# Experts' rows turned by DMA as 16-bit halves, in a mixture-of-experts kernel

## The chip, the cores and the metric

The kernel runs on one core of one Trainium2 chip. The metric is the device time of a run in microseconds; three runs of the kernel before gave 998.57, 999.82 and 1000.01, median 999.82. A core has TensorE (PE; matmuls, into PSUM), VectorE (DVE), ScalarE (ACT), GpSimd (POOL) and SyncE (SP), which here only issues transfers. ScalarE and GpSimd issue transfers as well. All transfers of the core share 16 DMA engines.

## The reference

Inputs are x and ctx, each 8 x 256 tokens of 512 values in float32. Two residual blocks follow one another:

```
x = x + attention(layernorm(x), ctx, ctx)      # 32 heads of 16, keys and values in 8 groups
h = layernorm(x)
logits = h @ gate_w.T                          # 32 experts
w, sel = the 4 largest logits per token, their softmax weights scaled to sum 1
large  = sum over the 4:  w * (silu(h @ Wg) * (h @ Wu)) @ Wd          # inner size 192
small  = sum over the 4:  w * (silu(h @ cWg) * (h @ cWu)) @ cWd       # inner size 128, one per two experts
x = x + large + 0.05 * small
```

The reference computes every expert for every token and weights most results with 0. The kernel computes each expert for the tokens that chose it alone: 2,048 tokens x 4 choices.

## The kernel before, in words

There are two stages, in float32 throughout.

**Attention** (up to about 490 us in the profile) runs over 8 batches of 256 tokens in slots of some 3 us, 16 to a batch. Within a slot TensorE makes a tile of scores (`scores`), the transposed scores of a tile ten slots earlier (`soft`), and one or two steps of other work that a table (`slots`) writes out by hand: projections, mixing of values, the output layer, and for each tile of 128 finished tokens layernorm, router and place in the experts' lists (`finish`). `InOrder` wraps TensorE, VectorE and ScalarE, so that their instructions keep the written order; steps put into `later` are issued at the next slot (`put_off`). In `finish`, `scale` leaves a tile of normed tokens in `row`; a slot later ScalarE's queue stores it to `xn_all` in DRAM, a table of rows from which experts gather, and `turn_h` turns it on TensorE for the router. GpSimd scatters each token's entries (row number, weight) into the lists of its four experts (L601).

**Two experts ahead.** Near the end of attention the two experts with most tokens so far are chosen, and their first 256 tokens of batches 0 to 5 are gathered (`gather_ahead`, L722) and computed (`ahead`) as filling between the last steps of attention. `turn` there turns 128x128 blocks on TensorE into PSUM and copies them to SBUF.

**The experts** (from about 490 us) come one after another, ordered by load, each with a fixed number of tokens (`SHARES`: 128 and 160, then 352 falling to 192). For expert i the steps are:

- `list_of` (L1055) loads the expert's list, `weights_of` loads 1.25 MB `wm` (L1041) and 0.75 MB `sm` (L1049); all are issued by SyncE. Four expert's weights fit (`wts`, four buffers).
- `tokens_of` (L1067) has GpSimd gather the listed rows, 128 to a tile, two or three tiles, into `rows` (three buffers).
- `turned` (L1094) turns the rows on TensorE: four chunks of 128 columns, for each two or three 128x128 blocks side by side in PSUM (`ept`), which VectorE (L1100) and ScalarE (L1098) in turns copy to `exT`. The chunks of expert i+1 are called between the products of expert i (`between` in `inner`).
- `inner` (L1114) makes five products of width w (gate, up, the tail of both, and the small expert's two), each of four matmuls, with Silu on ScalarE and multiplication on VectorE.
- `down` makes the second layer (L1217, L1219, L1222, for last tiles of few tokens L1195 to L1208), scales by the token's weight, and GpSimd adds the rows onto the output in DRAM (L1176). `in_turn` makes an expert's scatter-adds wait for those of the expert before.

The loop asks in iteration i for rows of i+3, weights of i+3 and the list of i+4. Here a scheduler, not the written order, decides how these instructions stand in SyncE's and GpSimd's queues. In the built program SyncE's queue repeats: wm of n, sm of n, list of n+1. A last loop (`For_i`) takes tokens beyond the fixed shares; there are none or few.

Of the kernel before, what the change touches and what calls it, by code (L numbers as in the profile page):

```python
# [10 lines left out]
F32 = mybir.dt.float32  # L11
I32 = mybir.dt.int32
U32 = mybir.dt.uint32
AF = mybir.ActivationFunctionType
# [22 lines left out]
WARM = 24  # L37
MAXT = B * S
NO_ONE = NS * P


class InOrder:
# [23 lines left out]
def xattn_moe(ctx: ExitStack, tc, x, ctxT, wqT, wkT, wvT, wfcT, bfc, gateT, wx, ws, out):  # L66
# [89 lines left out]
    with ExitStack() as att:  # L156
# [329 lines left out]
        def finish(t):  # L486
# [12 lines left out]
            def fc(h):  # L499
                half = slice(h * (E // 2), (h + 1) * (E // 2))  # L500
                pm = ps_m.tile([P, E // 2], F32, tag="pm", name=f"pmf_{t}_{h}")
                for kc in range(KC):
                    pe.matmul(
                        pm,
                        lhsT=box["oT"][:, kc, :],
                        rhs=wfc_sb[:, kc, half],
                        start=(kc == 0),
                        stop=(kc == KC - 1),
                    )
                dve.tensor_tensor(acc[t][:, half], pm, acc[t][:, half], ALU.add)  # L510
                if h == 0:
                    return
                row = box["row"] = a3.tile([P, E], F32, tag="row", name=f"row_{t}")

                def stats():
                    of = statistics(acc[t], f"f{t}")
                    act.dma_start(out=out[NO_ONE + t * P :][:P], in_=acc[t])

                    def scale():
                        scaled(row, acc[t], of)  # L520
                        later.append(
                            lambda: act.dma_start(out=xn_all[NO_ONE + t * P :][:P], in_=row)
                        )

                    later.append(scale)

                later.append(stats)
# [189 lines left out]

        def gather_ahead():
            for n in range(AHEAD):
                rows = [b2.tile([P, E], F32, tag=f"xn{j}", name=f"ahead{n}_{j}") for j in range(2)]  # L720
# [9 lines left out]
                first_ones["rows", n] = rows  # L730

        def ahead(n):


            a, at, b = units[n]
            up, us, wa, wt, wb = first_ones["weights", n]
            rows, li = first_ones["rows", n], first_ones["li", n]
            half = KC // 2
            xT = [ax.tile([P, half, S], F32, tag="acc", name=f"xT_ahead{n}_0")]

# [5 lines left out]
            steps = {}  # L746

            def turn(kc):
                pm = ps_m.tile([P, S], F32, tag="pm", name=f"pmt_ahead{n}_{kc}")
                for j in range(2):  # L750
                    pe.transpose(
                        pm[:, j * P : (j + 1) * P], rows[j][:, kc * P : (kc + 1) * P], ident
                    )
                dst = xT[kc // half][:, kc % half, :]

                if n or kc % 2:
                    act.copy(dst, pm)
                else:
                    dve.tensor_copy(dst, pm)

            def sum_of(name):

# [174 lines left out]
        for s in range(16 * B + LAG + 6):  # L937
# [16 lines left out]
            if s == 18:  # L954
                fill_blanks()

                hold(nc.sync.dma_start(
                    out=lists.rearrange("(e n) c -> e n c", e=NE)[:, :NO_ONE, :], in_=no_one
                ))
                hold(nc.sync.dma_start(  # L960
                    out=lists.rearrange("(e n) c -> e n c", e=NE)[:, NO_ONE : NO_ONE + S, :],
                    in_=no_one[:, :S, :],
                ))
                hold(nc.sync.dma_start(
                    out=xn_all[:NO_ONE, :].rearrange("(j p) r -> p j r", p=P),
                    in_=nothing.unsqueeze(1).to_broadcast([P, NS, E]),
                ))
            if s in do_ahead:
                do_ahead[s]()
# [65 lines left out]
    ps_x = ctx.enter_context(tc.tile_pool(name="ps_x", bufs=2, reuse_waits="tile", space=bass.MemoryType.PSUM))  # L1035
    ps_u = ctx.enter_context(tc.tile_pool(name="ps_u", bufs=3, reuse_waits="tile", space=bass.MemoryType.PSUM))
    ps_y = ctx.enter_context(tc.tile_pool(name="ps_y", bufs=3, reuse_waits="tile", space=bass.MemoryType.PSUM))

    def weights_of(e_r, n, after=None):
        wm = wts.tile([P, 5 * E], F32, tag="wm", name=f"wm_{n}")  # L1040
        load = nc.sync.dma_start(out=wm, in_=wx[bass.ds(e_r, 1), :, :].rearrange("o p n -> (o p) n"))  # L1041
        if after is not None:
            tc.add_manual_dep(
                load.ins, after.ins.name,
                mybir.DependencyInfo(mybir.DependencyClass.Sync, mybir.DependencyReason.DATA),
                reason="the rows before go first",
            )
        sm = wts.tile([P, 3 * E], F32, tag="sm", name=f"sm_{n}")
        loads.append(nc.sync.dma_start(out=sm, in_=ws[bass.ds(e_r, 1), :, :].rearrange("o p n -> (o p) n")))  # L1049
        return wm, sm  # L1050
# [10 lines left out]

    gathers = {}

    def tokens_of(li, n, ns):
        rows = m3.tile([P, NS, E], F32, tag="rows", name=f"rows_{n}")
        for j in range(ns):
            gathers[n] = nc.gpsimd.indirect_dma_start(  # L1067
                out=rows[:, j, :],
                out_offset=None,
                in_=xn_all,  # L1070
                in_offset=bass.IndirectOffsetOnAxis(ap=li[:, j, 0:1].bitcast(I32), axis=0),
            )
        return rows

    def tiles_of(w):

# [7 lines left out]
            lots[j] = "second" if j % 2 else "first"  # L1084
        return list(zip(sizes, lots))

    def turned(n, rows, ns):

        xT = m2.tile([P, KC, NS * P], F32, tag="xT", name=f"exT_{n}")

        def chunk(kc):
            pt = ps_x.tile([P, NS * P], F32, tag="pt", name=f"ept_{n}_{kc}")
            for j in range(ns):
                tensor.transpose(  # L1094
                    pt[:, j * P : (j + 1) * P], rows[:, j, kc * P : (kc + 1) * P], ident
                )
            if kc % 2:
                nc.scalar.copy(xT[:, kc, : ns * P], pt[:, : ns * P])  # L1098
            else:
                nc.vector.tensor_copy(xT[:, kc, : ns * P], pt[:, : ns * P])  # L1100

        return xT, chunk

# [207 lines left out]

    def fetch_weights(i):
        if i < NE:
            held["weights", i] = weights_of(held["expert", i], i, gathers[1] if i == 2 else None)

    def fetch_tokens(i):
        if i < NE:
            held["tokens", i] = tokens_of(held["list", i], i, ns_of[i])

    before = []  # L1320

# [36 lines left out]
    fetch_tokens(0)  # L1358
    with behind(held["lists", 2]):
        fetch_weights(0)  # L1360
    fetch_weights(1)
    fetch_tokens(1)
    fetch_weights(2)
    fetch_list(3)
    tensor = pe
    now = turned(0, held["tokens", 0], ns_of[0])
    for kc in range(KC):
        now[1](kc)

# [8 lines left out]
    for i in range(NE):  # L1378
        if i > 0:
            fetch_tokens(i + 3)  # L1380
        fetch_weights(i + 3)
        fetch_list(i + 4)
        wm, sm = held["weights", i]
        acts = units[i % 2]
        tensor = nc.tensor if i else pe
        if i + 1 < NE:
            then = turned(i + 1, held["tokens", i + 1], ns_of[i + 1])
# [12 lines left out]
    with tc.For_i(0, n_extra, 1) as i:  # L1400
# [4 lines left out]
        )  # L1405
        li = list_of(lists[bass.ds(row_r, P), :], "l", 1)
        wm, sm = weights_of(e_r, "l")
        rows = tokens_of(li, "l", 1)
# [6 lines left out]
        xT, chunk = turned("l", rows, 1)  # L1415
        for kc in range(KC):
            chunk(kc)
        inner("l", xT, wm, sm, units[0], P)
# [73 lines left out]
```

## Time and profile before

| what | value |
|---|---|
| median of the runs | 999.82 us |
| the profiled execution: its time, its span | 1007.55 us, 1005.7 us |
| mean granted TensorE clock over the span | 0.979 |
| TensorE busy | 971.5 us (97%), 5282 matmuls |
| VectorE, ScalarE, GpSimd busy | 414.3 us (41%), 316.0 us (31%), 321.2 us (32%) |
| the experts' turns: matmuls | 308 + 12, 54.1 + 3.0 us busy |
| copies of turned rows out of PSUM, VectorE, ScalarE | 64 each, 31.4 us and 27.1 us |
| gathers of rows | 80, GpSimd 78.6 us |
| scatter-adds to the output | 80, GpSimd 122.4 us |
| moved by DMA | 133.52 MB, mean 133 GB/s |

The profile gives the busy time of each engine; matmuls overlap in TensorE's pipeline, so their busy times add up to more than the time from one start to the next, and what a matmul costs is read from starts. In the timeline each row has its start and its duration in us, the engine (SPq is SyncE's queue of transfers), the line, the operation with what it writes and reads, and in brackets how long the engine sat idle ahead of it and what ended that. In a group of instructions, the figures after the bar are busy us and mean ns of one.

### The profile page before, as it was taken

What the parts mean: (1) busy time and instruction counts of PE and PEld (TensorE: products, weight loads), DVE (VectorE), ACT (ScalarE), POOL (GpSimd) and SP (SyncE); (2) the same over time, 40 slices, a digit from 0 to 9 for tenths busy, and PEclk for the clock granted to TensorE, in tenths of its full rate; (3) what the DMA queues carried; (4) which work ended last, traced back from release to release, by engine and by line L of the source; (5) the groups of instructions that cost most, each with busy time, mean ns of one, the idle gap of its engine ahead of it and who ended that gap; (6) DMA issues with size and microseconds to landing.
All of it is one profiled execution on the core that took longest, in us unless ns stands there. A gap on an engine that the chain in (4) does not pass through costs nothing. (4 is left out here: it accounts for less than half of the span.)

```text
span 1005.7 us, 14200 instructions
## 1 busy us (share of the span) xinstructions
PE 971.5 (97%) x5282; PEld 605.2 (60%) x5282; DVE 414.3 (41%) x958; ACT 316.0 (31%) x573; POOL 321.2 (32%) x333
## 2 busy tenths in 40 slices
PE   8999999999999998999889999999999999999994
PEld 5545555555555554438565556566767677777772
DVE  5655666666676667435212222222323222211220
ACT  2355455554454544422121122121212111111111
POOL 4201040413131303132426353443435434433322
PEclk9999999999999999959999999999999999999997
DMA  5120201011010000241698878676768687777722
GB/s 201 43 81 2 83 4 60 28 43 44 33 54 33 12 34 12 91 162 43 224 378 229 171 212 220 172 222 176 225 181 244 172 230 230 226 210 214 239 37 34
DMA packets 52632, 133.52 MB, mean 133 GB/s; under 512 B 19441, under 2 KB 20850, under 8 KB 48210
## 3 DMA queue, kind: packets, MB, share of 16 engines
q1 hardware_dynamic: 28690, 83.17, 24.1%
q0 software_dynamic: 18976, 40.25, 18.5%
q10 hardware_dynamic: 4896, 9.18, 2.4%
q8 instruction: 42, 0.69, 0.3%
q14 instruction: 28, 0.23, 0.1%
HBM read 104.75 MB, written 27.56 MB: 132 GB/s over the span
## 5 line engine op out<-in xcount | busy, mean ns | idle before, releaser
L52 DVE TENSOR_REDUCE mx<-sc 128x4 f32<-128x1024 f32 x128 | 156.6, 1223 | 79.3 <-PE st L52 67.0
L52 ACT ACTIVATE pT<-st 128x1024 f32<-128x1024 f32 x128 | 131.0, 1024 | 131.9 <-PE st L52 127.1
L1067 POOL DMA_INDIRECT rows<-xn_all,li x80 | 78.6, 983 | 235.6 <-DMA li<-lists 140.8
L52 PE MATMUL sc<-kT,qT 32*128 32x512 f32 x512 | 144.3, 640 | 5.9 <-DVE mx L52 5.4
L52 PE MATMUL st<-qT,k 32*128 32x512 f32 x512 | 148.0, 655 | 0.0
L1176 POOL DMA_INDIRECT out_dram<-y,li x80 | 122.4, 1530 | 70.2 <-ACT y L1174 40.5
L601 POOL DMA_INDIRECT lists<-ent,slot_i x64 | 62.5, 977 | 115.4 <-DVE slot_i L52 87.8
L1174 ACT ACTIVATE y<-py,li 128x512 f32<-128x512 f32 (+1 forms) x33 | 22.7, 687 | 182.0 <-PE py L1222 173.7
L1172 DVE TENSOR_SCALAR y<-py,li 128x512 f32<-128x512 f32 (+3 forms) x29 | 21.8, 750 | 116.6 <-PE py L1222 112.7
L1100 DVE COPY exT<-ept 128x384 f32<-128x384 f32 (+2 forms) x64 | 31.4, 491 | 90.5 <-PE ept L1094 80.4
L52 PEld LDWEIGHTS sc<-kT,qT 32*128 32x128 f32 x512 | 38.3, 182 | 44.6 <-DVE mx L52 21.2
L52 PE MATMUL po<-pT,va 128*32 128x512 f32 x512 | 65.0, 627 | 0.0
L52 PE MATMUL pmq<-xT,wq_sb 128*128 128x256 f32 x256 | 63.8, 392 | 0.8 <-DVE xT L52 0.8
L1114 PE MATMUL pu_g<-exT,wm 128*128 128x240 f32 (+10 forms) x248 | 63.9, 400 | 0.0
L52 PEld LDWEIGHTS pmq<-xT,wq_sb 128*128 128x128 f32 x256 | 46.0, 189 | 29.5 <-issue 23.5
L52 PE MATMUL pmf<-wfc_sb,oT 128*128 128x256 f32 x256 | 63.0, 391 | 0.0
L52 PEld LDWEIGHTS pmf<-wfc_sb,oT 128*128 128x128 f32 x256 | 46.2, 189 | 26.6 <-issue 15.2
L1114 PE MATMUL pu_ug<-exT,wm 128*128 128x240 f32 (+10 forms) x248 | 61.7, 393 | 0.0
L1114 PE MATMUL pu_u<-exT,wm 128*128 128x240 f32 (+10 forms) x248 | 60.9, 388 | 0.0
L1114 PE MATMUL pu_us<-exT,sm 128*128 128x240 f32 (+10 forms) x248 | 60.6, 387 | 0.0
L1114 PE MATMUL pu_gs<-exT,sm 128*128 128x240 f32 (+10 forms) x248 | 60.6, 387 | 0.0
L1219 PE MATMUL py<-sm,b 128*128 128x512 f32 x124 | 58.7, 593 | 0.3 <-DVE b L1142 0.3
(270 smaller groups left out, 1338.3 us busy)
## 6 DMA issues: line engine op xcount, KB each, us to landing
wm<-in_wx_dram SPq DMA_DIRECT2D x32, 1280.0 KB
sm<-in_ws_dram SPq DMA_DIRECT2D x32, 768.0 KB
out_dram<-acc ACTq DMA_DIRECT2D x16, 256.0 KB
xn_all<-row ACTq DMA_DIRECT2D x16, 256.0 KB
acc<-in_x_dram SPq DMA_DIRECT2D x15, 256.0 KB
ctx<-in_ctxT_dram SPq DMA_DIRECT2D x7, 512.0 KB
rows<-xn_all,li POOLq DMA_INDIRECT x80
out_dram<-y,li POOLq DMA_INDIRECT x80
```

The source lines that it names most:

```text
L52: this = instruction(*args, **kwargs)
L601: nc.gpsimd.indirect_dma_start(out=list_views[TOPK * t + k], out_offset=bass.IndirectOffsetOnAxis(ap=slot_i[:, k : k + 1], axis=0), in_=en ...
L1067: gathers[n] = nc.gpsimd.indirect_dma_start(out=rows[:, j, :], out_offset=None, in_=xn_all, in_offset=bass.IndirectOffsetOnAxis(ap=li[:, j ...
L1100: nc.vector.tensor_copy(xT[:, kc, : ns * P], pt[:, : ns * P])
L1114: tensor.matmul(pu[:, :w], lhsT=cols(kc), rhs=xT[:, kc, :w], start=(kc == 0), stop=(kc == KC - 1),)
L1172: nc.vector.tensor_scalar(y[:m], py[j][:m], weight(j)[:m], None, ALU.mult)
L1174: nc.scalar.activation(y[:m], py[j][:m], AF.Copy, scale=weight(j)[:m])
L1176: nc.gpsimd.indirect_dma_start(out=out, out_offset=bass.IndirectOffsetOnAxis(ap=li[:m, j, 0:1].bitcast(I32), axis=0), in_=y[:m], in_offset ...
L1219: nc.tensor.matmul(py[i], lhsT=b[:, s], rhs=wb, start=False, stop=False)
```

## The change

Everywhere that rows of experts are turned, DMA now does it. The DMA transposition handles 16-bit elements, so a float32 row is kept as its 512 lower halves followed by its 512 upper halves. Turned, each half is a matrix of its own, and a copy that writes with a stride of two 16-bit elements joins them to float32 again. Part by part:

- Router: ScalarE splits each tile of normed tokens (`split`, 128 x 1,024 16-bit elements) ahead of the store to `xn_all`, which becomes a table of 16-bit elements of the same size. `row` has two buffers, not three.
- Experts: `turn_halves` has SyncE issue one transposing transfer for each tile of rows, SBUF to SBUF, for w rows in all. `chunk` becomes one join from `halves` to `exT`, by VectorE and ScalarE in turns. TensorE's turns, PSUM between and their copies go.
- Gathers fetch the w rows of the share, not whole tiles of 128. `rows` has two buffers, `halves` two.
- The loop asks in iteration i for the turn of i+2, after the weights of i+3 and the list of i+4.
- The third expert's weights no longer wait for the second one's gathers by a dependency of their own.
- PSUM: one bank for turns in place of two, four for results in place of three.
- The two experts ahead are turned in the same way.

In the built program of the changed kernel, SyncE's queue repeats from the eighth expert on: wm of n, sm of n, list of n+1, the two or three turns of n+1, wm of n+1.

```diff
+def halves_of(a):
+    return a.bitcast(U16).rearrange("p (n two) -> p two n", two=2)
+
+def joined(copy, dst, turned, kc):
+    copy(halves_of(dst), turned.rearrange("p (two c) n -> p c two n", two=2)[:, kc])
...
-    xn_all = nc.dram_tensor("xn_all", (B * S + NO_ONE, E), F32, kind="Internal").ap()
+    xn_all = nc.dram_tensor("xn_all", (B * S + NO_ONE, 2 * E), U16, kind="Internal").ap()
...
-        a3 = att.enter_context(tc.tile_pool(name="a3", bufs=3))
+        a3 = att.enter_context(tc.tile_pool(name="a3", bufs=2))
...
-                        later.append(
-                            lambda: act.dma_start(out=xn_all[NO_ONE + t * P :][:P], in_=row)
-                        )
+                        def split():
+                            halves = a3.tile([P, 2 * E], U16, tag="halves", name=f"split_{t}", bufs=1)
+                            act.copy(
+                                halves.rearrange("p (two n) -> p two n", two=2), halves_of(row)
+                            )
+                            act.dma_start(out=xn_all[NO_ONE + t * P :][:P], in_=halves)
+                        later.append(split)
...
+                turned = first_ones["turned", n] = aq.tile(
+                    [P, 2 * KC, S], U16, tag=f"qT{n}", name=f"turned_ahead{n}"
+                )
+                for j in range(2):
+                    nc.sync.dma_start(
+                        out=turned[:, :, j * P : (j + 1) * P], in_=rows[j], transpose=True
+                    )
...
-                pm = ps_m.tile([P, S], F32, tag="pm", name=f"pmt_ahead{n}_{kc}")
-                for j in range(2):
-                    pe.transpose(
-                        pm[:, j * P : (j + 1) * P], rows[j][:, kc * P : (kc + 1) * P], ident
-                    )
...
+                copy = act.copy if n or kc % 2 else dve.tensor_copy
+                joined(copy, xT[kc // half][:, kc % half, :], halves, kc)
...
+    mh = ctx.enter_context(tc.tile_pool(name="mh", bufs=2, reuse_waits="tile"))
...
-    ps_x = ctx.enter_context(tc.tile_pool(name="ps_x", bufs=2, ...
+    ps_x = ctx.enter_context(tc.tile_pool(name="ps_x", bufs=1, ...
...
-    ps_y = ctx.enter_context(tc.tile_pool(name="ps_y", bufs=3, ...
+    ps_y = ctx.enter_context(tc.tile_pool(name="ps_y", bufs=4, ...
...
-    def tokens_of(li, n, ns):
-        rows = m3.tile([P, NS, E], F32, tag="rows", name=f"rows_{n}")
-        for j in range(ns):
+    def tokens_of(li, n, w):
+        rows = mh.tile([P, NS, 2 * E], U16, tag="rows", name=f"rows_{n}")
+        for j, (m, _) in enumerate(tiles_of(w)):
             gathers[n] = nc.gpsimd.indirect_dma_start(
-                out=rows[:, j, :],
+                out=rows[:m, j, :],
...
+    def turn_halves(rows, n, w):
+        halves = mh.tile([P, 2 * KC, NS * P], U16, tag="halves", name=f"halves_{n}")
+        for j, (m, _) in enumerate(tiles_of(w)):
+            nc.sync.dma_start(
+                out=halves[:, :, j * P : j * P + m], in_=rows[:m, j, :], transpose=True
+            )
+        return halves
...
         def chunk(kc):
-            pt = ps_x.tile([P, NS * P], F32, tag="pt", name=f"ept_{n}_{kc}")
-            for j in range(ns):
-                tensor.transpose(
-                    pt[:, j * P : (j + 1) * P], rows[:, j, kc * P : (kc + 1) * P], ident
-                )
-            if kc % 2:
-                nc.scalar.copy(xT[:, kc, : ns * P], pt[:, : ns * P])
-            else:
-                nc.vector.tensor_copy(xT[:, kc, : ns * P], pt[:, : ns * P])
+            copy = nc.scalar.copy if kc % 2 else nc.vector.tensor_copy
+            joined(copy, xT[:, kc, :w], halves[:, :, :w], kc)
...
         fetch_weights(i + 3)
         fetch_list(i + 4)
+        turn_tokens(i + 2)
```

More of the change, by code (lines that the diff above doesn't have):

```diff
@@ L13 @@
 U32 = mybir.dt.uint32
+U16 = mybir.dt.uint16
 AF = mybir.ActivationFunctionType
@@ L719, in gather_ahead @@
             for n in range(AHEAD):
-                rows = [b2.tile([P, E], F32, tag=f"xn{j}", name=f"ahead{n}_{j}") for j in range(2)]
+                rows = [
+                    b2.tile([P, 2 * E], U16, tag=f"xn{j}", name=f"ahead{n}_{j}") for j in range(2)
+                ]
                 for j in range(2):
@@ L729, in gather_ahead @@
                     )
-                first_ones["rows", n] = rows
+                turned = first_ones["turned", n] = aq.tile(
[5 more added lines that the diff above has]
+                    )
         def ahead(n):
@@ L736, in ahead @@
             up, us, wa, wt, wb = first_ones["weights", n]
-            rows, li = first_ones["rows", n], first_ones["li", n]
+            halves, li = first_ones["turned", n], first_ones["li", n]
             half = KC // 2
@@ L748, in turn @@
             def turn(kc):
-                pm = ps_m.tile([P, S], F32, tag="pm", name=f"pmt_ahead{n}_{kc}")
-                for j in range(2):
-                    pe.transpose(
-                        pm[:, j * P : (j + 1) * P], rows[j][:, kc * P : (kc + 1) * P], ident
-                    )
-                dst = xT[kc // half][:, kc % half, :]
-                if n or kc % 2:
-                    act.copy(dst, pm)
-                else:
-                    dve.tensor_copy(dst, pm)
+                copy = act.copy if n or kc % 2 else dve.tensor_copy
+                joined(copy, xT[kc // half][:, kc % half, :], halves, kc)
             def sum_of(name):
@@ L965, in xattn_moe @@
                     out=xn_all[:NO_ONE, :].rearrange("(j p) r -> p j r", p=P),
-                    in_=nothing.unsqueeze(1).to_broadcast([P, NS, E]),
+                    in_=nothing.bitcast(U16).unsqueeze(1).to_broadcast([P, NS, 2 * E]),
                 ))
@@ L1032, in xattn_moe, with weights_of @@
     m2 = ctx.enter_context(tc.tile_pool(name="m2", bufs=2, reuse_waits="tile"))
+    mh = ctx.enter_context(tc.tile_pool(name="mh", bufs=2, reuse_waits="tile"))
     m3 = ctx.enter_context(tc.tile_pool(name="m3", bufs=3, reuse_waits="tile"))
     m6 = ctx.enter_context(tc.tile_pool(name="m6", bufs=6, reuse_waits="tile"))
-    ps_x = ctx.enter_context(tc.tile_pool(name="ps_x", bufs=2, reuse_waits="tile", space=bass.MemoryType.PSUM))
+    ps_x = ctx.enter_context(tc.tile_pool(name="ps_x", bufs=1, reuse_waits="tile", space=bass.MemoryType.PSUM))
     ps_u = ctx.enter_context(tc.tile_pool(name="ps_u", bufs=3, reuse_waits="tile", space=bass.MemoryType.PSUM))
-    ps_y = ctx.enter_context(tc.tile_pool(name="ps_y", bufs=3, reuse_waits="tile", space=bass.MemoryType.PSUM))
-    def weights_of(e_r, n, after=None):
+    ps_y = ctx.enter_context(tc.tile_pool(name="ps_y", bufs=4, reuse_waits="tile", space=bass.MemoryType.PSUM))
+    def weights_of(e_r, n):
         wm = wts.tile([P, 5 * E], F32, tag="wm", name=f"wm_{n}")
[L1041 to L1046, printed above, removed]
-            )
+        nc.sync.dma_start(out=wm, in_=wx[bass.ds(e_r, 1), :, :].rearrange("o p n -> (o p) n"))
         sm = wts.tile([P, 3 * E], F32, tag="sm", name=f"sm_{n}")
@@ L1062, in xattn_moe @@
     gathers = {}
-    def tokens_of(li, n, ns):
-        rows = m3.tile([P, NS, E], F32, tag="rows", name=f"rows_{n}")
-        for j in range(ns):
+    def tokens_of(li, n, w):
+        rows = mh.tile([P, NS, 2 * E], U16, tag="rows", name=f"rows_{n}")
+        for j, (m, _) in enumerate(tiles_of(w)):
             gathers[n] = nc.gpsimd.indirect_dma_start(
-                out=rows[:, j, :],
+                out=rows[:m, j, :],
                 out_offset=None,
                 in_=xn_all,
-                in_offset=bass.IndirectOffsetOnAxis(ap=li[:, j, 0:1].bitcast(I32), axis=0),
+                in_offset=bass.IndirectOffsetOnAxis(ap=li[:m, j, 0:1].bitcast(I32), axis=0),
             )
         return rows
+    def turn_halves(rows, n, w):
[5 more added lines that the diff above has]
+        return halves
     def tiles_of(w):
@@ L1085, in tiles_of, with turned @@
         return list(zip(sizes, lots))
-    def turned(n, rows, ns):
+    def turned(n, halves, w):
         xT = m2.tile([P, KC, NS * P], F32, tag="xT", name=f"exT_{n}")
         def chunk(kc):
-            pt = ps_x.tile([P, NS * P], F32, tag="pt", name=f"ept_{n}_{kc}")
-            for j in range(ns):
-                tensor.transpose(
-                    pt[:, j * P : (j + 1) * P], rows[:, j, kc * P : (kc + 1) * P], ident
-                )
-            if kc % 2:
-                nc.scalar.copy(xT[:, kc, : ns * P], pt[:, : ns * P])
-            else:
-                nc.vector.tensor_copy(xT[:, kc, : ns * P], pt[:, : ns * P])
+            copy = nc.scalar.copy if kc % 2 else nc.vector.tensor_copy
+            joined(copy, xT[:, kc, :w], halves[:, :, :w], kc)
         return xT, chunk
@@ L1313, in fetch_weights, with turn_tokens @@
         if i < NE:
-            held["weights", i] = weights_of(held["expert", i], i, gathers[1] if i == 2 else None)
+            held["weights", i] = weights_of(held["expert", i], i)
     def fetch_tokens(i):
         if i < NE:
-            held["tokens", i] = tokens_of(held["list", i], i, ns_of[i])
+            held["tokens", i] = tokens_of(held["list", i], i, SHARES[i])
+    def turn_tokens(i):
+        if i < NE:
+            held["halves", i] = turn_halves(held["tokens", i], i, SHARES[i])
     before = []
@@ L1360, in xattn_moe @@
         fetch_weights(0)
+    turn_tokens(0)
     fetch_weights(1)
     fetch_tokens(1)
+    turn_tokens(1)
     fetch_weights(2)
@@ L1365, in xattn_moe @@
     tensor = pe
-    now = turned(0, held["tokens", 0], ns_of[0])
+    now = turned(0, held["halves", 0], SHARES[0])
     for kc in range(KC):
@@ L1386, in xattn_moe @@
         if i + 1 < NE:
-            then = turned(i + 1, held["tokens", i + 1], ns_of[i + 1])
+            then = turned(i + 1, held["halves", i + 1], SHARES[i + 1])
             inner(i, now[0], wm, sm, acts, SHARES[i], then[1])
@@ L1407, in xattn_moe @@
         wm, sm = weights_of(e_r, "l")
-        rows = tokens_of(li, "l", 1)
+        rows = tokens_of(li, "l", P)
         ed = m1.tile([P, 1], F32, tag="led", name="led")
@@ L1414, in xattn_moe @@
         )
-        xT, chunk = turned("l", rows, 1)
+        xT, chunk = turned("l", turn_halves(rows, "l", P), P)
         for kc in range(KC):
```

## Prediction

> **What bounds the kernel now.** I read the profile in this order: the 40 slices of the span, the groups of instructions, then the timeline of one expert on TensorE, SyncE and GpSimd. The slices first (busy tenths, granted TensorE clock, DMA share):
>
> ```profile
> PE   8999999999999998999889999999999999999994
> PEclk9999999999999999959999999999999999999997
> DMA  5120201011010000241698878676768687777722
> ```
>
> TensorE is full from end to end. The DMA engines are idle in attention (the first 19 slices) and 60 to 80% busy in the experts' stage (from about slice 20, 490 us), full only at its start. The chain of waits is cut off after 2 us and tells nothing. The group to be removed, and the stage (TensorE's busy time, weight loads, DVE, ScalarE, GpSimd, clock, DMA share, GB/s):
>
> ```profile
> L1094 PE MATMUL ept<-ident,rows 128*128 128x128 f32 x308 | 54.1, 275 | 2.4 <-DMA rows<-xn_all,li 2.4
> ```
>
> ```profile
> 700.00:800.00 100.00, 100.00 (x534) 66.74 (x532) 26.80 (x66) 19.49 (x48) 43.03 (x34) 1.00 0.71 203
> ```
>
> 100 of 100 us: here a turn saved on TensorE is time saved. One expert of 288 tokens, TensorE first, then SyncE's queue, then GpSimd:
>
> ```profile
> 706.38 0.49 PE L1094 MATMUL ept<-ident,rows 128*128 128x128 f32 x3
> 706.71 2.11 PE L1114 MATMUL pu_u<-exT,wm 128*128 128x288 f32 x8
> ```
>
> ```profile
> 706.55 0.33 SPq L1041 DMA_DIRECT2D wm<-in_wx_dram  x1
> 707.24 0.18 SPq L1049 DMA_DIRECT2D sm<-in_ws_dram  x1
> 709.86 0.01 SPq L1055 DMA_DIRECT2D li<-lists  x1
> 722.96 0.33 SPq L1041 DMA_DIRECT2D wm<-in_wx_dram  x1
> ```
>
> ```profile
> 717.54 1.02 POOL L1067 DMA_INDIRECT rows<-xn_all,li  x1 [7.55 <-DMA li<-lists]
> 718.87 0.98 POOL L1067 DMA_INDIRECT rows<-xn_all,li  x1 [0.30 <-issue]
> 720.15 0.95 POOL L1067 DMA_INDIRECT rows<-xn_all,li  x1 [0.30 <-issue]
> 721.41 1.62 POOL L1176 DMA_INDIRECT out_dram<-y,li  x1 [0.30 <-issue]
> ```
>
> Two things are to be seen. Three turns push the next matmul back by only 706.71 - 706.38 = 0.33 us, 0.109 each; the 275 ns of the group overlap. And SyncE issues one expert's two weight loads (2 MB) and the next expert's list, then waits for nothing but a free weight buffer. The list lies behind the weights: it lands 717.54 - 706.55 = 11.0 us after wm's issue, and GpSimd gathers then. That latency is no bound today, since SyncE does not wait for it.
>
> **What is removed.** 308 + 12 turns of experts x 0.109 = 34.8 us of TensorE. 24 of them (experts 0 to 2) lie at 494 to 518 us, where TensorE waits for rows and weights anyway, so 296 x 0.109 = 32.2 us could show. The 16 turns of the two experts taken ahead fill waits of TensorE for DVE's routing; I take 1 us. Gathers shrink from 80 x 128 = 10,240 rows to 8,352, 3.9 MB less.
>
> **What is added, off the path.** The joins handle twice as many elements (608 for 304 tokens). ScalarE's rows (0.48 us for 384, 1.02 for 1,024 elements) give about 0.67 us for 0.48, DVE's (0.56 for 384, 1.22 for 1,024) about 0.78 for 0.56. DVE and ScalarE are 27% and 19% busy and a join is needed only by the next expert: nothing. Without that cover it would be 128 x 0.2 = 26 us. The split in attention is 16 copies of 1,024 elements on ScalarE, 1.02 us each by the exponential's row. In the slot where it falls ScalarE has 0.5 to 1 us idle and is half busy over attention; bounds 0 and 16 us, and I take 2, because the copies behind it are read a slot or more later. The turns of the ahead experts are behind their weights, which land by 437 us; TensorE needs them at 451: nothing, or up to 5 us if a turn is dear. PSUM is only regrouped (8 banks as before): nothing.
>
> **What is added on the path: a wait in SyncE's queue.** In the built order of the changed kernel, SyncE's queue from the eighth expert's weights on repeats: wm and sm of expert n, list of n+1, *two or three turns of n+1*, wm of n+1. The turn of n+1 waits for n+1's gather, that for n+1's list, and the list lies behind wm and sm of n. So the next weights are no longer released by a free buffer but by a ring of latencies. (With rows and halves two deep, a turn also waits for the joins of n-1, and a gather for the turns of n-1; both are done a ring earlier. The wait that holds the third expert's weights behind a gather goes, but the turns ahead of them wait for the same gather. On GpSimd the gather of n+1 stands ahead of the scatter-adds of n-3; six result tiles cover that.) The ring:
>
> - wm to the landing of the list: 11.0 us above; in other experts 11 to 14 (754.89 to 768.51, 859.91 to 872.18). The higher ones have gathers of the same moment in them, which the ring now puts before wm; the scatter-adds still overlap. I take 10.8 (10.5 with two tiles), and 0.5 for turns still ahead in the queue.
> - list to the last gather's landing: the third is issued at +3.56 us (721.10 - 717.54); from the end of an issue to the landing I take the routing scatter's 2.45 us (issue ends 398.56, its waiter starts at 401.01). First gather +3.5, second +4.8, third +6.0.
> - the turns themselves, X us for 128 x 1,024 halves (256 KB). No row shows one. Below: a plain issue, 0.33 us. Above: the Trainium skill, "VectorE: DVE Perf Modes", The three transpose paths, puts a 128x128 turn of 16-bit data at 1309 ns by DMA against 390 on TensorE; eight blocks are 10.5 us. This rule speaks against the change doubly, since the trace has TensorE at 109 ns a block, not 390. At 1309 ns in series 8,352 rows would be 65.25 x 8 x 1.309 = 683 us, more than the whole stage of 510. "DMA: Bandwidth & Descriptors", Latency and other measured facts, says 261 GB/s for such transposes: 1.0 us a piece, 17.1 MB in 65 us, and 0.71 share of DMA has room for it. A lone transfer's 1309 ns hold its latency (over 2 us in the rows here), so they are hardly a rate; I estimate X = 1.5, near the bandwidth figure, with 0.33 and 10.5 kept.
>
> With X = 1.5 the turns of three tiles start at +3.5, +5.0, +6.5 (the last short) and end at +7.1: ring = 10.8 + 0.5 + 7.1 + 0.3 for SyncE's own steps = 18.7 us. Two tiles: 10.5 + 0.5 + 6.4 + 0.3 = 17.7. TensorE alone would need 16.6 - 1.3 = 15.3 and 13.7 - 0.8 = 12.8. The ring is longer than either, so it sets the pace once the lead of four weight buffers is eaten (about two experts' time).
>
> Its sum: wm of the eighth expert (566 before) goes out at about 574, because its turn waits for joins in the fifth expert. Then 11 rings of three tiles and 13 of two: 574 + 206 + 230 = 1010 for the last weights (941 before). They land 9 us later[...]; the last expert took from 980.2 to the end at 1005.7, 25.5, now 24.5. End: 1043.5, less 1 from the ahead experts, plus 2 from the split: 1044.5 of span. The profiled execution is 1007.55 us for a span of 1005.7, and the median of the runs, 999.82, is 7.7 below it: 1044.5 + 1.85 - 7.7 = 1039, rounded to 1040. What is late next is TensorE, for weights at each expert's first product.
>
> **Rivals.**
>
> *The ring is short enough (not slower).* If list and gathers land faster, since the DMA engines now have idle time within each ring, TensorE stays the bound. Place: wm to the list. The ring decides at 16.5 us on average ((971 - 574) / 24 makes the last expert start where it does now); at 15.2 the whole 32 us show. With X = 0.33 and the list after 9 us the rings are 15.8 and 14.3. Then span 1005.7 - 32.2 - 1 + 2 + 3 for the crowded start = 977.5, median 972. For it: my latencies come from crowded moments. Against it: no wm of the trace had its list in under 11 us.
>
> *Turns are dear.* With X = 3.2 (the geometric middle of 1.0 and 10.5, some 80 GB/s) the rings are 22.5 and 20.9: 574 + 10 for the start + 247 + 272 + 33.5 = 1137, median about 1131. With 10.5 they are 38 and 34, over 1450. For it: the 1309 ns. Against: the bandwidth figure.
>
> *ScalarE's split stalls attention* at its full 16 us with everything else as forecast: 1054. Against: idle time around it.
>
> *The change does not do what it says*: TensorE keeps no expert turn in the built program, so this is out.
>
> **How the numbers follow.** Ring with X of 0.7 to 2 (1010 to 1065): 0.45. Dear turns (1075 and up): 0.25, of it 0.10 above 1150. Ring about even with TensorE: 0.05 within 0.2% (some 2 us, about what a measurement of this kernel tells from no change) and 0.05 just above. TensorE-bound (970 to 997): 0.20, of it 0.10 below 980. So 980 to 1150 leaves out 0.2; faster 0.20, same 0.05, slower 0.75.
>
> **What would show it.** Right: SyncE's waits name the gather (DMA rows) ahead of the turns; distances from wm to wm are 17 to 19 us from the eighth expert on and equal list plus gather plus turns; TensorE falls below 9 tenths from about 650 us on, waiting for DMA wm at an expert's first product; the DMA share falls though bytes rise. Wrong on the ring: wm still waits for TensorE's last product of an expert. Wrong on X: successive turns of one expert start much more, or less, than 1.5 us apart. Wrong on the split: the end of attention moves by over 5 us.

## The result, and the profile after

The changed kernel takes 1089.52 us (median of 4 runs, 1083.95 to 1094.28), the kernel before 999.2 in the same comparison: the ratio is 1.0902, with a 95% interval of 1.0849 to 1.0955. The prediction said slower and 1040; the time is inside its range, but the loss is more than twice the forecast one (90 us for 40). The profiled execution took 1088.9 us, for a span of 1087.1. Of the 42 runs of the kernel before beside the experiments, 7 took 1005.5 to 1008.2 us and the others 997.7 to 1001.8, and the profiled execution of before (1007.55) is one like the 7.

The slices of the changed kernel, to be laid beside those of before (busy tenths, granted clock, DMA share; a slice is 27.2 us here):

```profile
PE   8999999999999999987879999978878878887774
PEclk9999999999999998998889999999899989888888
DMA  5120102020200005439998886876786878686862
```

Up to slice 26, about 700 us, TensorE is as full as before outside the start of the experts' stage. From there on it never is again. In the window of 700 to 800 us (TensorE, weight loads, DVE, ScalarE, GpSimd, clock, DMA share, GB/s) it works 79.55 of 100 us, where it worked 100, its granted clock is 0.90 for 1.00, and the DMA share is 0.76 for 0.71:

```profile
700.00:800.00 100.00, 79.55 (x364) 51.56 (x361) 19.77 (x54) 17.67 (x39) 34.36 (x28) 0.90 0.76 186
```

One expert in SyncE's queue, from its weights to the next one's, and the gathers on GpSimd that lie between (start, duration in us):

```profile
747.23 0.52 SPq L1062 DMA_DIRECT2D wm<-in_wx_dram  x1
747.94 1.31 SPq L1064 DMA_DIRECT2D sm<-in_ws_dram  x1
750.77 0.39 SPq L1070 DMA_DIRECT2D li<-lists  x1
762.43 5.06 SPq L1094 DMA_TRANSPOSE halves<-rows  x3
767.75 0.48 SPq L1062 DMA_DIRECT2D wm<-in_wx_dram  x1
```

```profile
758.84 1.02 POOL L1082 DMA_INDIRECT rows<-xn_all,li  x1 [11.66 <-DMA li<-lists]
760.16 0.98 POOL L1082 DMA_INDIRECT rows<-xn_all,li  x1 [0.30 <-issue]
761.45 0.86 POOL L1082 DMA_INDIRECT rows<-xn_all,li  x1 [0.30 <-issue]
```

This is the ring of the prediction, closed: wm at 747.23, the list behind it lands at 758.84, gathers, three turns from 762.43 to 767.49, and only then the next wm at 767.75, 20.5 us later. Before, the next wm came 16.4 us after the last (706.55 to 722.96). The waits tell the same. In SyncE's queue, and on the other engines (engine, line, what was waited for: us in total, times, longest):

```profile
SPq L1094 <- DMA rows<-xn_all,li: 265.1, 31, 13.4
```

```profile
ACT exT L50 <- DMA halves<-rows: 297.8, 26, 15.9
POOL rows L1082 <- DMA li<-lists: 268.6, 25, 13.4
DVE exT L50 <- DMA halves<-rows: 250.8, 26, 14.2
...
PE pu_gs L1131 <- ACT sg L1139: 79.8, 20, 7.6
```

SyncE waits for gathers, GpSimd for lists, and ScalarE and VectorE for turned rows, each for over 250 us: one circle. TensorE's own wait is named last. It stands at its fourth product (`pu_gs`), since that needs a PSUM buffer which ScalarE's Silu has to empty, and this Silu stands behind a join that waits for turned rows. The weights themselves are never late. SyncE, for its part, hardly waits for TensorE: 4.9 us in all for weight buffers that TensorE still reads.

What a turn does to SyncE's queue is read from its line (count: least, median, most ns):

```profile
L1094 SPq DMA_TRANSPOSE halves<-rows x80: 1204/1399/5926, 485.5 to 1041.4; - x80
```

And what the turns cost the DMA engines is read from the queue that SyncE fills (packets, MB, share of 16 engines' time):

```profile
q1 hardware_dynamic: 101730, 101.33, 32.3%
```

Before, it had 28,690 packets, 83.17 MB and 24.1%. So 18.2 MB more take 73,040 packets of 249 bytes, and 0.323 x 1087.1 - 0.241 x 1005.7 = 109 us of all 16 engines.

### The profile page after: what moved, and what is told of

Its sections match the earlier page's. It is cut to its first block, busy times and chain, and to the rows that moved or that the text cites. A ratio compares the mean times of both kernels' runs of the same rounds, so it can differ in the third digit from the quotient of the medians.

```text
span 1087.1 us, 13724 instructions
## 1 busy us (share of the span) xinstructions
PE 964.4 (89%) x4946; PEld 591.5 (54%) x4946; DVE 406.9 (37%) x958; ACT 347.3 (32%) x589; POOL 322.3 (30%) x333
## 5 line engine op out<-in xcount | busy, mean ns | idle before, releaser
L63 ACT ACTIVATE pT<-st 128x1024 f32<-128x1024 f32 x128 | 131.3, 1025 | 119.5 <-PE st L63 119.3
L1131 PE MATMUL pu_gs<-exT,sm 128*128 128x240 f32 (+10 forms) x248 | 86.8, 510 | 79.8 <-ACT sg L1139 79.8
L50 ACT COPY exT<-halves 128x480 uint16<-128x480 uint16 (+11 forms) x64 | 45.2, 771 | 306.1 <-DMA halves<-rows 297.8
L50 DVE COPY exT<-halves 128x480 uint16<-128x480 uint16 (+11 forms) x64 | 25.9, 458 | 250.8 <-DMA halves<-rows 250.8
L1131 PEld LDWEIGHTS pu_gs<-exT,sm 128*128 128x128 f32 x248 | 59.1, 249 | 101.3 <-ACT sg L1139 88.0
L1131 PE MATMUL pu_us<-exT,sm 128*128 128x240 f32 (+10 forms) x248 | 68.4, 424 | 0.0
L1131 PEld LDWEIGHTS pu_us<-exT,sm 128*128 128x128 f32 x248 | 54.5, 222 | 12.8 <-issue 0.4
```

Of the source, the lines that this page charges most:

```text
L50: copy(halves_of(dst), turned.rearrange("p (two c) n -> p c two n", two=2)[:, kc])
L63: this = instruction(*args, **kwargs)
L1131: tensor.matmul(pu[:, :w], lhsT=cols(kc), rhs=xT[:, kc, :w], start=(kc == 0), stop=(kc == KC - 1),)
```

## The experiments

The theory: the ring of latencies in SyncE's queue (weights, list, gather, turn, next weights) takes the time. Its rivals: joins that stand in order on ScalarE and VectorE ahead of work for TensorE; DMA engines that the turns fill; the turning itself. Each experiment is one edit to the changed kernel, unless it says otherwise. The runs of before beside them have medians of 999.7 to 1000.5.

**The turn moved behind the next weights and list.**

```diff
-        turn_tokens(i + 2)
+        with behind(held["lists", min(i + 4, NE - 1)]):
+            turn_tokens(i + 2)
```

> The changed kernel, with each expert's turns held in SyncE's queue where the loop writes them: the turn of i+2 after the weights of i+3 and the list of i+4. Its gather is then an expert old when SyncE comes to it. Ring theory (the next weights wait for list, gather and turn of the same expert, 20.6 us a round with three tiles and 17.7 with two): the ring is gone, TensorE is the bound again, less its turns: 965 to 985 us. Bandwidth theory (the turns' small packets fill the DMA engines): still 1040 us or more, DMA share near 1 through the experts' stage. In-order theory (joins stand ahead of Silu in ScalarE's order and stop TensorE): 1060 us or more.

Measured: 1017.8 us (1012.47 to 1023.35), ratio 1.0173 [1.0148, 1.0197]. Of the loss of 90 us, 72 are gone with an edit that changes nothing but the place of the turns in one queue. SyncE's wait for gathers falls from 265.1 to 31.2 us, and wm waits for TensorE again. So the ring carries most of the loss. But 18 us are left and TensorE's saving does not show; none of the three expectations gave this time. The reading that offered itself, DMA engines full of turns (their share was 1.12 to 1.15 from 550 to 900 us), is tried below with turns that nobody waits for, and full engines alone do not give the 18 us.

**Plain copies in place of turns**, in the same place, with the same bytes and the same wait. The rows are not turned, so the kernel computes with wrong rows.

```diff
-            nc.sync.dma_start(
-                out=halves[:, :, j * P : j * P + m], in_=rows[:m, j, :], transpose=True
-            )
+            move = nc.sync.dma_start(
+                out=halves[:, :, j * P : j * P + m],
+                in_=rows[:, 0, :].rearrange("p (c n) -> p c n", n=P)[:, :, :m],
+            )
+            tc.add_manual_dep(move.ins, gather_of[n][j].ins.name, ...
```

> The changed kernel with each experts' turn replaced by a plain copy of the same size from SBUF to SBUF, issued by SyncE at the same place and after the same gather; the rows are not turned (the computation leaves that out, and takes all tiles from the first one). Ring theory: only the turns' issue time leaves the ring, some 2.2 us of 20.6 with three tiles and 1.6 of 17.7 with two, and their data ahead of the weights some 0.5: 1025 to 1045 us, so most of the loss stays. Bandwidth theory, or one in which turning by itself is what costs: 1000 us or less.

Measured: 1042.85 us (1041.42 to 1043.28), ratio 1.0429 [1.0413, 1.0445]. The ring is there without any turning (SyncE waits 196.5 us for gathers), and it costs 43 us. The other 47 come with the turning. A plain copy holds SyncE's queue 0.61 us (median), a turn 1.40, so one would expect 11 rings of three tiles x 2.4 us and 13 of two x 1.6, together 47. The sum meets the total, but by luck: of the 46 us between the two spans 13.9 lie ahead of the eighth expert's weights, 11.5 in the eleven rings of three tiles (19.5 us each for 20.5), 19.5 in the thirteen of two (16.3 for 17.8) and 1.0 at the end.

**All joins written behind the fifth product**, so that no Silu should stand behind a join.

```diff
-        between(0)
...
-        between(3)
...
+        for kc in range(KC):
+            between(kc)
```

> The changed kernel with the four joins of the next expert put after an expert's fifth product, not between its products, so that no Silu stands behind a join that waits for its turn. Ring theory: the wait only moves to the next expert's first product and the pace stays; at the end the last but one expert need not wait for the last turn, 8 to 10 us: about 1080 us. In-order theory: the stall goes, 1000 to 1020 us.

Measured: 1089.92 us, ratio 1.0905 [1.088, 1.0929], no difference from the changed kernel. But the edit did not reach the engines. In the built program the joins stand where they stood: from 485 us on ScalarE's 222 instructions and VectorE's 289 come in the same order as in the changed kernel. The next expert's joins (544 elements) still stand ahead of this expert's Silu (288), and TensorE waits 81.2 us for it, where it waited 79.8:

```profile
731.24 1.46 ACT L50 COPY exT<-halves 128x544 uint16<-128x544 uint16 x2 [12.31 <-DMA halves<-rows]
...
734.02 0.41 ACT L1139 ACTIVATE sg<-pu_g 128x288 f32<-128x288 f32 x1
```

So this run is the changed kernel once more and does not test the rival. What speaks against it lies elsewhere. The members of the ring hardly wait for the engines that compute (SyncE 4.9 us in all for TensorE to free weight buffers and 7.4 for ScalarE, GpSimd's scatter-adds 10.2 for ScalarE), and the kernel with the list first and ten buffers, below, has the joins in the same place ahead of the Silu and runs at TensorE's pace. TensorE's wait for ScalarE is where the delay is felt, not where the pace comes from. The 8 to 10 us that a later join might save at the end stay untested.

**The list asked for ahead of the weights.**

```diff
-        fetch_weights(i + 3)
         fetch_list(i + 4)
+        fetch_weights(i + 3)
```

> The changed kernel with the list of i+4 asked for ahead of the weights of i+3, so that no list lies behind 2 MB of weights; the turns still stand ahead of the next weights in SyncE's queue. Ring theory: the largest term of the ring (11.7 us from the weights to the list's landing) falls to 2 or 3, the ring to 11 to 14 us, below TensorE's 12.8 to 15.3: 965 to 990 us. Bandwidth theory: still 1040 us or more. In-order theory: 1060 us or more.

Measured: 1046.05 us (1041.76 to 1053.53), ratio 1.0452 [1.0427, 1.0477]: half of the loss is back, where the ring theory had wanted all. SyncE's largest wait in the experts' stage shows why:

```profile
SPq L1070 <- DMA out_dram<-y,li: 239.5, 30, 11.9
```

The list now waits for one of six list buffers, which is free when the scatter-adds of an earlier expert are done. A new wait took the place of the old one, and the rings are still 18.7 and 15.8 us on the average.

**The same with ten list buffers, and ten list buffers alone** (`tc.tile_pool(name="ls", bufs=10)`).

> e4_list_first (the list asked for ahead of the weights in the loop; 1046.05) with ten list buffers in place of six. There the list waited 239.5 us for the scatter-adds that free a list. If that wait is what kept the ring at 16 to 18.4 us, the list now goes out early, the ring is gone, and the time comes to that of the late turn: 1005 to 1025 us. If it is the turns' and gathers' own latency: 1040 to 1050 us.

> The changed kernel with ten list buffers in place of six and the order of its queues as it was: the control to e7_list_first_deep, which has ten buffers and the list ahead of the weights (986.19). In the changed kernel no list waits for a buffer; it waits for its place behind weights and turns. If that place is the cause, ten buffers alone give nothing: 1083 to 1096 us. If depth of lists by itself had brought the gain: below 1040 us.

Measured, as a table of the two edits (median us, ratio to before with its interval):

| | six list buffers | ten list buffers |
|---|---|---|
| order as changed | 1089.52, 1.0902 [1.0849, 1.0955] | 1091.80, 1.087 [1.0792, 1.0947] |
| list ahead of the weights | 1046.05, 1.0452 [1.0427, 1.0477] | **986.19, 0.9859 [0.9812, 0.9906]** |

Buffers alone give nothing; the order alone gives half; both give a kernel that is faster than the changed one by 103 us and than the kernel before by 13.5. The expectation of 1005 to 1025 was too modest. One period of this kernel in SyncE's queue, and its pace on TensorE (first products of two experts of 288 tokens; then the same two products in the kernel before):

```profile
719.55 0.39 SPq L1070 DMA_DIRECT2D li<-lists  x1
728.39 3.93 SPq L1094 DMA_TRANSPOSE halves<-rows  x3
732.58 1.39 SPq L1062 DMA_DIRECT2D wm<-in_wx_dram  x1
```

```profile
701.59 2.21 PE L1131 MATMUL pu_g<-exT,wm 128*128 128x288 f32 x8
...
716.90 2.21 PE L1131 MATMUL pu_g<-exT,wm 128*128 128x288 f32 x8
```

```profile
704.34 2.21 PE L1114 MATMUL pu_g<-exT,wm 128*128 128x288 f32 x8
...
720.97 2.21 PE L1114 MATMUL pu_g<-exT,wm 128*128 128x288 f32 x8
```

The queue looks the same as in the changed kernel, list, turns, weights. The difference is whose list it is: the turn at 728.39 uses rows that were gathered from 715.65 on, with a list issued at 704.29. List, gather and turn of an expert now spread over more than one expert's time, and nothing in the queue waits for what stands just ahead of it. The pace is TensorE's own, 15.31 us, where it was 16.63 before (704.34 to 720.97): 12 turns saved 1.32 us, 0.110 each.

Why 13.5 us and not 32? From the seventh expert's start to the last one's this kernel saves 27.3 us. But it comes to the seventh expert late, at 604.91 us, where the kernel before with idle turns (below, 1000.62 us, the same attention) starts it at 592.29.

**The late turn with plain copies.** The first two edits together.

> The late turn (behind the list of i+4, as in e1_turn_late), with each turn replaced by a plain copy of as many bytes from SBUF to SBUF, which waits for the same gather. The turning itself is left out, so the experts work on wrong rows. e1_turn_late took 1017.8 with TensorE held up, though the ring was gone. If what is left there is the DMA engines' time that turning takes (q1 73.6% against 38.7% before in 700 to 900 us), plain copies free it and the 32 us of TensorE show: 965 to 990 us. If it is the waits for two buffers of rows and halves and the later joins, it stays: 1010 to 1025 us. In between: both.

Measured: 979.5 us, ratio 0.9789 [0.9759, 0.9818]. So buffers and joins, which are as in the late turn, do not by themselves hold that kernel at 1018; the turning does, in that place. By what, the next two narrow down.

**The late turn with three buffers of rows and of halves** (`tc.tile_pool(name="mh", bufs=3, ...)`).

> e1_turn_late with three buffers of rows and of halves in place of two. If the waits for buffers hold it up (GpSimd waited 221.6 us for turns to free rows before its gathers in e1_turn_late), the time falls to 970 to 995 us. If the DMA engines are full with turns, a buffer more only moves the waiting: 1010 to 1025 us.

Measured: 1022.24 us, ratio 1.0208 [1.0177, 1.0239]. GpSimd's 221.6 us of waiting for rows to be turned were not the bound.

**The kernel before with turns that nobody waits for.**

```diff
+        if i + 2 < NE:
+            with behind(held["lists", min(i + 4, NE - 1)]):
+                turn_idle(i + 2)
```

> The kernel before, unchanged on TensorE, with the 74 turns of experts 2 to 31 added on SyncE's queue behind the list of i+4; they turn a constant tile into a tile that nobody reads, and wait for no gather. This is the turns' DMA work alone, without ring, joins or fewer rows. If that work is what is left in e1_turn_late, the experts' stage becomes bound by DMA here too, at about e1's 1018 plus some of the 3.9 MB of longer gathers: 1015 to 1040 us. If the DMA engines had room for it, as I forecast: 999 to 1006 us.

Measured: 1000.62 us (12 runs), ratio 0.9989 [0.9967, 1.001]. The trace has 77 turns with 16.5 MB and a mean DMA share of 1.03 from 550 to 950 us (0.76 before), and TensorE does not notice (columns as in the window above):

```profile
550.00:950.00 400.00, 400.00 (x1856) 268.48 (x1856) 95.53 (x227) 76.35 (x177) 164.67 (x130) 1.00 1.03 248
```

Weights, lists and gathers do have room beside the turns, so "full of turns" does not explain the 18 us of the late turn, and 986.19 above, at a share of 0.98 to 1.07, says so again. What is left is latency. With the turns behind 2 MB of weights, one holds the queue 2.73 us (median; up to 7.61) for 1.28 in the kernel with the list first, where they go out after the weights have passed. In the late turn 16 to 21 us go by from wm's issue to the first join with turned rows in the experts of 640 to 850 us, more than the 15.3 that TensorE needs for one; with plain copies it is 14 to 17. I infer that this is the bound there; no run measures it by itself.

**Turns issued by ScalarE, with two buffers and with three.**

```diff
-        turn_tokens(i + 2)
+        turn_tokens(i + 2, nc.scalar)
```

> The changed kernel with the turns of experts 2 to 31 issued by ScalarE, between its last Silu and its first scaling of an expert, in place of SyncE. SyncE's queue then holds weights and lists alone, as before. This takes the turns out of the ring, and also out from behind the 2 MB of weights, which in e1_turn_late stand ahead of them in the same queue (there 17 to 21 us passed from wm's issue to the turned rows' landing, and an expert takes TensorE 13 to 15). If the place behind the weights is what was left in e1_turn_late (1017.8), the saving of TensorE shows: 968 to 990 us. If turning itself is too slow, whatever its queue: 1010 to 1030 us. If ScalarE's wait for the gather, ahead of its own work, takes the ring's place: above 1040 us.

> e11_act_queue with three buffers of rows and of halves in place of two. If gathers wait for turns to free their rows in e11_act_queue, this is 5 to 15 us faster than it; if DMA engines or ScalarE bind it, within 3 us of it. A version to beat the kernel before would have to come in at 990 us or less.

Measured: 1120.42 us, ratio 1.1193 [1.1138, 1.1247], and 1110.21, ratio 1.1084 [1.1018, 1.115]. Both are the slowest of all, as the third expectation had it, but not for its reason: the wait is for the issue, not for a gather. ScalarE in the first of them:

```profile
780.27 9.48 ACTq L1094 DMA_TRANSPOSE halves<-rows  x3
789.86 0.69 ACT L1191 ACTIVATE y<-py,li 128x512 f32<-128x512 f32 x1 [14.03 <-issue]
```

```profile
ACT y L1191 <- issue: 160.3, 12, 15.1
```

Three turns, begun 0.5 us after the weights' issue at 779.81, hold ScalarE for 9.48 us, and the scaling of a result, for which TensorE's buffers wait, stands behind them. Over the kernel ScalarE idles 160.3 us at that place while it issues; its waits for gathers ahead of turns come to 9. An issue of a turn is not free for the engine that issues it; SyncE, which computes nothing, is the better place.

**The kernel before with gathers of w rows only**, the one part of the change that needs no turning by DMA. TensorE turns `rows[:m]` with `ident[:m, :m]`.

> The kernel before with one part of the change alone: gathers fetch the w rows of the share, not whole tiles of 128, and TensorE turns and the engines copy only those. TensorE turns 8,352 columns for 10,240, some 59 of 308 turns less if a turn's time goes with its rows: 59 x 0.109 = 6.4 us, so 991 to 996 us. If a turn has a fixed price, only 3.9 MB of DMA go, which TensorE does not wait for: 998.5 to 1001 us.

Measured: 1018.7 us, ratio 1.0177 [1.0153, 1.02]: slower by 18.2, where I had expected a gain or nothing. A group of three turns, the last of 32 rows, and the product after it:

```profile
711.05 0.56 PE L1094 MATMUL ept<-ident,rows 128*128 128x128 f32 x3
711.53 2.21 PE L1114 MATMUL pu_u<-exT,wm 128*128 128x288 f32 x8
...
713.58 0.56 PE L1094 MATMUL ept<-ident,rows 128*128 128x128 f32 x3
```

The weight loads (PEld) of the short turn and of the product behind it:

```profile
711.36 0.13 PEld L1094 LDWEIGHTS ept<-ident,rows 32*128 32x128 f32 x1 [0.17 <-issue]
711.53 0.54 PEld L1114 LDWEIGHTS pu_u<-exT,wm 128*128 128x128 f32 x3
```

The group takes 711.53 - 711.05 = 0.48 us where whole tiles took 0.33, and the product 2.05 where it took 1.94. This group costs about 0.26 us more, four times an expert. Over the stage, groups of three whose last tile has 16 to 64 rows step by 0.49 us (median; 0.33 before), groups of two, with a last tile of 80 to 112 rows, by 0.18 to 0.21 (0.22 before), and the one with 64 rows by 0.40. TensorE is busy and its clock full throughout, so it is its own time. The trace shows where it goes: a weight load usually starts together with the matmul ahead of it and is hidden behind it, and so it is here for last tiles of 80 rows and more. For 16 to 64 rows it starts only 0.20 us after the start of that matmul, and the next product's load 0.17 us after the short one, so two loads stand in the open. Why the short ones are not hidden, the trace does not show.

## Why the prediction was half right

**The mechanism was right.** The ring was named with its members and its place, and three runs that break it (late turn, list first, list first with buffers) give back 72, 43 and 103 us. Three of the signs asked for came: SyncE's waits name the gather, the distances from wm to wm are the sum of list, gather and turns, TensorE falls below 9 tenths. That fall came at 700 us and not 650: until the thirteenth expert's start at 701.67 TensorE ran on its lead and at its new pace, 16.51 us an expert for 17.83.

**The removed turns were right**: 0.110 us each against 0.109. With the list first, the time from the seventh expert's start to the last one's shrinks from 380.4 to 353.1 us.

**The size was wrong, in these terms** of the sum 574 + 206 + 230 + 33.5 (span 1044.5, measured 1087.1):

| term | forecast | measured | difference |
|---|---|---|---|
| wm of the eighth expert | 574 | 582.45 | +8.5 |
| 11 rings of three tiles | 206 (18.7 each) | 225.7 (20.5) | +20 |
| 13 rings of two tiles | 230 (17.7) | 231.3 (17.8) | +1 |
| last wm to the end of the span | 33.5 | 47.7 | +14 |
| less 1 ahead, plus 2 for the split | +1 | not seen | -1 |
| from the span to the median | -4.5 | +2.4 | +7 |

The turns of the ring shown above, one by one:

```profile
762.43 1.30 SPq L1094 DMA_TRANSPOSE halves<-rows  x1
763.82 1.27 SPq L1094 DMA_TRANSPOSE halves<-rows  x1
765.18 2.30 SPq L1094 DMA_TRANSPOSE halves<-rows  x1
```

- *Three tiles.* The step that failed is "The turns of three tiles start at +3.5, +5.0, +6.5 (the last short) and end at +7.1", in its last clause: the short turn was put at 0.6 us and took 2.30. The turns start at +3.6, +5.0 and +6.3 after the list's landing at 758.84, as forecast, and end at +8.65. The two whole tiles hold the queue 1.30 and 1.27 us (X was taken as 1.5), the last one, of 16 rows, 2.30. In the eleven rings of three tiles the last turn takes 1.79 to 3.20 us, in the median 2.30: 1.7 us too much, 11 times, are 19 of the 20 us. The list's part was 11.6 for 11.3. With the list first and six buffers most last turns of 16 to 48 rows take 1.17 to 1.24 us and whole tiles 1.27, so rows do not set the price. Why the last turn of a ring costs a microsecond more in the changed kernel stays open. GpSimd's scatter-adds are under way beside it there and not in the other kernel, but no run separates that.
- *Two tiles.* That this term came out to 1 us is in part luck. The first eight of these rings took 18.3 us on the average, since the last turn was dear here too (1.77 to 2.80 us); in the last five the second turn of three experts slipped behind that expert's own weights, and they took 16.9.
- *Start.* I had the eighth expert's weights wait for one turn. Eight turns stood ahead of them in the queue and filled 566.43 to 582.25. The sum also left out that the first expert waits for its turn: TensorE stands 9.29 us before its first product, which starts at 495.31 us, for 489.16 in the kernel before with idle turns. With the list first and ten buffers it starts at 494.96: nearly half of the 12.6 us by which that kernel comes late to its seventh expert.
- *End.* I counted landing and computing of the last expert. But its second turn stands behind its own weights in the queue: it goes out at 1041.43, and the joins start at 1050.15. ScalarE does these joins ahead of the Silu of the expert before, so TensorE waits 7.26 us in that expert too, and the last one starts at 1061.63.
- *The offset* belongs to the start. The 566 us, and so the 574, were read in an execution of before that had lost some 7 us to its clock by then (granted clock 0.50 from 440 to 450 us), and taking 7.7 off at the end made up for that. The changed kernel's profiled execution has no such loss: it lies 0.6 below its median. Without it the forecast start is 567, and the start is what was off, by some 15 us.

**Readings that failed without moving the sum.** TensorE was to wait for weights at the first product; it waits for turned rows, at the fourth. The DMA share was to fall; it rose from 0.71 to 0.76, since turns take 109 us of the engines for the 65 that I estimated from the 261 GB/s of the Trainium skill's page "DMA: Bandwidth & Descriptors" (section Latency and other measured facts): 18.2 MB in 109 us are 167 GB/s. That there is room for them all the same was right, as the idle turns in the kernel before show. The 1309 ns a block of the Trainium skill's page "VectorE: DVE Perf Modes" (section The three transpose paths) are no rate here: the 65.25 x 8 blocks took the engines 109 us, 0.21 a block. The split moved nothing: attention's last output product starts at 453.31 us, for 454.26 in the kernel before with idle turns. A join costs 0.46 us on VectorE and 0.77 on ScalarE (0.78 and 0.67 estimated), and is hidden.

**The rivals.** "The ring is short enough" is out for this order of the queue, but its mechanism is what the list ahead of the weights brings about: that kernel takes 986. "Dear turns" is out as to X of a whole tile, though turning in place of plain copying is 47 of the 90 us, two thirds of it inside the rings. What stays open is the 18 us of the late turn, the dear last turn of a ring and why short turns on TensorE do not hide their loads.

## What to carry to other kernels

When a step that waits is put into a queue that only issued before, follow one round of the queue and ask whether anything in it waits for something that stands just ahead of it in the same queue; if so, its latencies add up to a period, and an engine's saved work is worth nothing until that period is shorter than the engine's own. The cure is order and depth together: ask for the head of the chain (a 3 KB list) ahead of the bulk (2 MB of weights), and give its buffers enough depth to be asked for early, since either alone leaves a wait. Count transfers, not bytes, for what a turn costs the queue. Before a run is read as a test of an order, look in its trace whether the order changed.

## What the runs showed that I had not expected

- A turn of up to 128x1,024 16-bit elements from SBUF to SBUF holds the queue of its engine 1.2 to 1.3 us in most turns of the kernel with the list first and six buffers, whether it has 16 rows or 128. The last turn of a ring of the changed kernel holds it 1.70 to 3.20. A plain copy of the same bytes holds it 0.61 in the same place. Behind 2 MB of weights in the same queue both are dearer: 2.73 and 1.29 us (medians), up to 7.61 for a turn; on ScalarE up to 10.51.
- Turns move in packets of some 249 bytes, 110 to 167 GB/s by the time of the engines (165 us in the late turn, 109 in the changed kernel, for 18.2 MB).
- A mean DMA share of 1.03 over 400 us did not slow a kernel whose transfers are asked for early enough (1000.62 with 77 idle turns for 1000.46).
- On TensorE a turn of 16 to 64 rows behind whole tiles costs more than a whole one (0.49 us a group for 0.33, and some 0.1 in the product after it), because its weight load and the next one do not overlap the matmul ahead; the kernel before with short turns is 18.2 us slower.
